# A four-layer attention network on one core: the input of the next image's layer 1 is loaded while layer 3 finishes, into a tile outside the pools that later holds similarities

## The chip, the cores and the metric

The kernel runs on one core of one Trainium2 chip. Its engines are TensorE (PE, the matmuls, with weight loads shown as PEld), VectorE (DVE), ScalarE (ACT), GpSimd (POOL) and SyncE (SP, which here only issues DMAs). The metric is the time of one execution on the device, in microseconds, smaller is better.

## The reference

The input is four images of 32 x 32 positions with 384 channels in fp32. Each image goes through four layers of the same form, `x = x + layer(gn(x))`, where gn is a group norm over 32 groups of 12 channels:

```python
x = x + _L0_conv_ref(_gn(x), ...)   # deformable attention, 6 heads of 64
x = x + _L1_conv_ref(_gn(x), ...)   # attention with group weights, 12 heads of 32
x = x + _L2_conv_ref(_gn(x))        # ratio of box sums
x = x + _L3_conv_ref(_gn(x), ...)   # outlook attention over 3 x 3 patches
```

What the change touches lies in layers 1 and 3. Layer 1 multiplies the softmax of each head by a matrix of group weights, `sim @ sim^T`, where `sim = sigmoid(...)` of the normalized products of the features xg with their strided convolution gc. Layer 3 computes nine attention vectors of nine weights for each position, applies them to the values of the 3 x 3 neighbours and folds the results back onto the image:

```python
v = image @ Wv + bv
attn = softmax((image @ Wa + ba).reshape(B, H, W, 9, 9))
win = einsum('bhwpq,bhwqc->bhwpc', attn, patches)    # patches: 3x3 windows of v
out = fold(win)                                      # 9 shifted adds
```

## The kernel before

**Two lanes.** `Front` computes layer 0, `Trunk` layers 1 to 3. Layer 0 of image 0 runs alone (about 640 us). Then `Net.layer3` (L271) drives both: the trunk works on image b and the front on image b+1. Each lane is a generator whose yields carry a number of steps; after each yield of the trunk the front is advanced until its share of the work is ahead by 0.1. This sets the order in which the program is written down. Engines take their instructions in an order that a scheduler derives from that, from the dependences and from the buffers, each engine in its own fixed order, and waits between engines are semaphores. The trunk of image 3 has no front beside it.

**Buffers.** Tiles of SBUF come from pools. `scope` opens a pool for a stretch of code; when it ends, its space is given to the next pool on that side, and whatever writes there first waits for the last reader or writer of the old tiles, transfers included. Channels stand on the 128 partitions, in KC = 3 slices of N = 1024 positions; NJ = 8 is the number of blocks of 128 positions. PSUM has two buffers `big` (1024 columns) and four `bank` (512). Weights of 384 x 384 go round in three buffers `w`.

**Norm.** `norm` (L314) takes the statistics of each slice on DVE (`stats`, L301), then sums over groups with a constant matrix gmat on PE: 14 matmuls of one column for the mean (gn_mv, L330), four small operations on DVE (L340 to L347), 14 more for the variance (gn_d, L330), Sqrt on ACT (L349), a reciprocal (L352), and the three slices of the result (L357). The dense products that follow are `dense_t` (L376, out channels on partitions) and `dense_n` (L390, positions on partitions).

**Layer 1.** `Trunk.image` (L828) opens the pool l1y (tiles q4, k4, xg), `layer1` (L838) the pool l1, in which `pair_tiles` (L975) zeroes parts of the pair tiles on POOL (L986 to L989), and then l1a for `inputs1` (L848): x is loaded by SP (L852) from x1, where the front stored it, and normed into a second tile xh. After that come the features xg (whose pads POOL zeroes at L862), queries, keys and values, which are written to DRAM, and the sums of the first pair of heads (`sums_step`, L1026; `sums_finish`, L1052, which copies a row `lrow` and stores it as `lse`, L1063). The pool l1b then holds the work of the six pairs: `sims` (L1065) computes the similarities by matmuls L1074 and sigmoids L1081 into a tile sim of 16 KB a partition; `pair` (L1090) scales them on POOL (sg, L1139), multiplies keys by queries (L1154), exponentiates (L1162), and multiplies sg by sim (L1184). `gf`/`gn` tiles keep parts for a later transpose.

**Layers 2 and 3.** `layers23` (L1217) opens the pool l23 with its own tile x, loaded by ACT's queue (L1227) from x1 again and added to layer 1's result. Layer 2 (L1256) has a tile d for each slice (L1292). Layer 3 (L1354) norms into xh, computes attention and values (L390), gathers the folded weights with selection matmuls (L1415), and writes each block's 5 x 5 window weights through DRAM (skew, L1449) so that they come back as a banded matrix mt (L1451); even blocks on SP, odd ones on ACT. Meanwhile PE transposes x in eight groups (L1460) and ACT copies each group into a tile y of its own (L1464). At the end 22 passes, the products of mt with the values (L1472, two records each in the trace), are added to y on DVE (L1480), and SP stores the eight blocks of the output (L1481). Then the next image begins.

**Front beside the seam.** Where the front works on the next image, its stores of sampled pairs (L555), dense products (L376) and grouped convolutions (L584) stand between the trunk's instructions on all engines. POOL gathers for it (L652).

The lines that set the order at the end of layer 3 and the start of layer 1:

```python
            for i in range(NJ):
                pt = self.big()
...
                y = self.wt([P, C], "y", NJ)
                nc.scalar.copy(y, pt[:, 0:C])
                ys.append(y)
            yield 20
            for i in range(NJ):
...
                nc.sync.dma_start(out[i * P : (i + 1) * P, :], y)
```

Of the kernel before, what the change touches and what calls it, by code (L numbers as in the profile page):

```python
# [26 lines left out]
P = 128  # L27
NB, HW, C = 4, 32, 384
N = HW * HW
KC = C // P  # L30
NJ = N // P
# [41 lines left out]
class Net:  # L73


    def __init__(self, ctx, tc, a):
        self.tc, self.nc, self.a = tc, tc.nc, a
        nc = self.nc
        pool = lambda name, bufs, **kw: ctx.enter_context(
            tc.tile_pool(name=name, bufs=bufs, **kw)  # L80
        )
        self.const = pool("const", 1)
        self.wts = pool("wts", 3)
        self.ps2 = pool("ps2", 2, space=PSUM)
        self.ps1 = pool("ps1", 4, space=PSUM)
        self.dram = pool("dram", 1, space=DRAM)
        self.n = 0
        self.consts()
        self.scratch()
        self.front, self.trunk = Front(self, "right"), Trunk(self, "left")  # L90

    def nm(self, base):
        self.n += 1
# [186 lines left out]
class Lane:  # L280
# [30 lines left out]
        self.stat = self.work  # L311
        return self.wt([P, KC, 2], "gn_mv", 2)

    def norm(self, x, out, mv=None):  # L314


        nc = self.nc
        if mv is None:
            mv = self.moments()
            for k in range(KC):  # L320
                self.stats(mv, x, k)
        gmat = self.weights("gmat")

        near = [[k for k in range(KC) if abs(k - ko) <= 1] for ko in range(KC)]

        def groups(src):
            ps = self.bank()
            for ko in range(KC):
                for ki in near[ko]:
                    nc.tensor.matmul(  # L330
                        ps[:, ko : ko + 1],
                        gmat[:, ki, ko * P : (ko + 1) * P],
                        src[:, ki, :],
                        start=ki == near[ko][0],
                        stop=ki == near[ko][-1],
                    )
            return ps[:, 0:KC]

        mean = self.wt([P, KC], "gn_mean")
        nc.vector.tensor_scalar(mean, groups(mv[:, :, 0:1]), 1.0 / 12.0, None, ALU.mult)  # L340
        d = self.wt([P, KC, 1], "gn_d")
        d2 = d.rearrange("p k o -> p (k o)")
        m0 = mv[:, :, 0:1].rearrange("p k o -> p (k o)")
        v0 = mv[:, :, 1:2].rearrange("p k o -> p (k o)")
        nc.vector.tensor_tensor(d2, m0, mean, ALU.subtract)
        nc.vector.tensor_tensor(d2, d2, d2, ALU.mult)
        nc.vector.tensor_tensor(d2, d2, v0, ALU.add)  # L347
        rstd = self.wt([P, KC], "gn_rstd")
        nc.scalar.activation(  # L349
            rstd, groups(d), AF.Sqrt, bias=self.eps[:, 0:1], scale=1.0 / 12.0  # L350
        )
        nc.vector.reciprocal(rstd, rstd)  # L352
        for k in range(KC):
            src = x[:, k, :]
            if len(out.shape) == 4:
                src = src.rearrange("p (y x) -> p y x", y=HW)
            nc.vector.tensor_scalar(  # L357
                out[:, k],
                src,
                mean[:, k : k + 1],  # L360
                rstd[:, k : k + 1],
                ALU.subtract,
                ALU.mult,
            )
# [460 lines left out]
class Trunk(Lane):  # L825


    def image(self, b, out):  # L828
        with self.scope("l1y"):


            self.q4, self.k4 = self.wt([P, N], "q4"), self.wt([P, N], "k4")
            self.xg = self.wt([P, N], "xg")
            yield from self.layer1(b)
            yield from self.layers23(b, out)
# [11 lines left out]

    def inputs1(self, b):  # L848
        nc, v = self.nc, self.nc.vector
        x = self.wt([P, KC, N], "x")  # L850
        for k in range(KC):
            nc.sync.dma_start(x[:, k, :], self.x1[b % 2][k * P : (k + 1) * P, :])  # L852
        xh = self.wt([P, KC, N], "xh")
        self.norm(x, xh)
        yield 15


        pads, raw = [], self.wt([P, KC, M1], "raw")
        w = self.weights("Wg")
# [52 lines left out]
        for k in range(KC):  # L912
            out = slice(32 * k, 32 * k + 32)
# [5 lines left out]
            for ps, src in ((psx[:, 0:512], 0), (psx[:, 512:N], 512), (psc[:, 0:M1], N)):  # L919
# [4 lines left out]
                    start=True,  # L924
# [18 lines left out]
        for k in range(KC):  # L943
            rows, heads = slice(k * P, (k + 1) * P), slice(32 * k, 32 * k + 32)
            ps, pc = self.big(), self.bank()
            for out, lo in ((ps[:, 0:512], 0), (ps[:, 512:N], 512), (pc[:, 0:M1], N)):
# [4 lines left out]
                    start=True,  # L951
# [113 lines left out]
    def sims(self, p):  # L1065

        nc = self.nc
        sim = self.wt([P, 2, 2, N], "sim")
        for h in range(2):
            for m in range(2):  # L1070
                ps = self.big().rearrange("p (r n) -> p r n", r=2)
                for r in range(2):
                    rows = slice(64 * r, 64 * r + 64)
                    nc.tensor.matmul(  # L1074
                        ps[:, r, :],
                        self.gc[rows, m * P : (m + 1) * P],
                        self.xg[rows, h * 512 : (h + 1) * 512],
                        start=True,
                        stop=True,
                    )  # L1080
                nc.scalar.activation(  # L1081
                    sim[:, :, m, h * 512 : (h + 1) * 512],
                    ps,
                    AF.Sigmoid,
                    bias=self.rows[:, R_SCAL + 1 : R_SCAL + 2],
                    scale=self.rows[:, R_SCAL : R_SCAL + 1],
                )
        return sim
# [127 lines left out]

    def layers23(self, b, out):  # L1217
        with self.scope("l23"):
            self.x = self.wt([P, KC, N], "x")
            yield from self.out1(b)  # L1220
            yield from self.layer2()
            yield from self.layer3(b, out)
# [33 lines left out]
    def layer2(self):  # L1256
        nc, v = self.nc, self.nc.vector
        with self.scope("l2"):
# [8 lines left out]
            def squares(k):  # L1267


                sq = self.wt([P, HW, HW + 4], "sq", 3)  # L1270
                nc.scalar.activation(sq, xp[:, k], AF.Square)

                two = self.wt([P, HW, HW + 2], "t", 2)
                v.tensor_tensor(two, xp[:, k, :, 0 : HW + 2], xp[:, k, :, 1 : HW + 3], ALU.add)
                ps = self.big()
                for h in range(2):
                    rows = slice(16 * h, 16 * h + 16)
                    for i, src in enumerate(
                        (two[:, rows, 0:HW], two[:, rows, 2 : 2 + HW], xp[:, k, rows, 4 : 4 + HW])
                    ):  # L1280
                        nc.tensor.matmul(
                            ps[:, h * 512 : (h + 1) * 512],
                            self.ident,
                            src,
                            start=i == 0,
                            stop=i == 2,
                        )
                s = self.wt([P, N], "s", KC)
                nc.scalar.activation(s, ps, AF.Square)
                num.append(s)  # L1290
                t = self.wt([P, HW, HW + 2], "t", 2)
                d = self.wt([P, HW, HW], "d", KC)  # L1292
                v.tensor_tensor(t, sq[:, :, 0 : HW + 2], sq[:, :, 1 : HW + 3], ALU.add)
                v.tensor_tensor(d, t[:, :, 0:HW], t[:, :, 2 : HW + 2], ALU.add)
                v.tensor_tensor(d, d, sq[:, :, 4 : HW + 4], ALU.add)
                for lo in (0, HW - 2):
                    e = d[:, :, lo : lo + 2]
                    v.tensor_tensor(e, e, bc(self.wnorm[:, lo : lo + 2], 1, HW), ALU.mult)
                den.append(d.rearrange("p y x -> p (y x)"))
# [54 lines left out]
    def layer3(self, b, out):  # L1354
        nc, v = self.nc, self.nc.vector
        skew = self.skew[b % 2]
        with self.scope("l3"):
# [95 lines left out]
                )  # L1453

            values(range(NJ // 2, NJ))
            ys = []
            for i in range(NJ):
                pt = self.big()
                for k in range(KC):
                    nc.tensor.transpose(  # L1460
                        pt[:, k * P : (k + 1) * P], self.x[:, k, i * P : (i + 1) * P], self.ident
                    )
                y = self.wt([P, C], "y", NJ)
                nc.scalar.copy(y, pt[:, 0:C])  # L1464
                ys.append(y)
            yield 20
            for i in range(NJ):
                ps = self.bank()
                near = [j for j in range(NJ) if abs(i - j) <= 1]
                for j in near:  # L1470
                    c0 = P * (i - j) + P
                    nc.tensor.matmul(  # L1472
                        ps[:, 0:C],
                        mt[:, j, c0 : c0 + P],
                        vals[:, j, :],
                        start=j == near[0],
                        stop=j == near[-1],
                    )
                y = ys[i]
                v.tensor_tensor(y, ps[:, 0:C], y, ALU.add)  # L1480
                nc.sync.dma_start(out[i * P : (i + 1) * P, :], y)  # L1481
                yield 4
# [84 lines left out]
```

## Time and profile before

| what | value |
| --- | --- |
| time, median of 3 runs | 4876.06 us (4868.23 to 4881.34) |
| the profiled execution: time | 4831.1 us |
| the profiled execution: span from first to last instruction | 4829.3 us |
| mean granted clock of TensorE in it | 0.91 of full speed |
| busy in the span: PE, PEld, DVE, ACT, POOL | 4189.8, 1799.4, 3132.9, 2404.9, 946.3 us |
| data moved by DMA | 366.82 MB |

The profile is of one execution. Times in it count from its first instruction. An engine's busy time is the time in which one of its instructions runs; for PE the ends of matmuls are modelled, so a busy PE can be slow. The chain of waits is followed back from the last instruction: at each step to what released it, or to the instruction before it on the same engine; a row gives start, length, engine, the tile written, the line and a count of instructions. "issue" is time in which an engine waited for nothing that the profile shows. `PEclk` is the granted clock of TensorE in tenths, in forty equal slices of the span.

By stretches of the span, PE is busy and its mean granted clock is:

| stretch, us | what | PE busy, us | clock |
| --- | --- | --- | --- |
| 0-640 | layer 0 of image 0 alone | 361.05 | 0.75 |
| 640-1787 | image 0's trunk, image 1's front | 1043.31 | 0.93 |
| 1787-1853.4 | seam 0 to 1 | 62.43 of 66.4 | 0.87 |
| 1853.4-2926.9 | image 1's trunk, image 2's front | 985.13 | 0.93 |
| 2926.9-2993.35 | seam 1 to 2 | 62.34 of 66.45 | 0.87 |
| 2993.35-4041 | image 2's trunk, image 3's front | 962.19 | 0.94 |
| 4041-4072.5 | seam 2 to 3 | 20.09 of 31.5 | 0.77 |
| 4072.5-4829.3 | image 3's trunk alone | 693.21 | 0.94 |

### The profile page before, as it was taken

The page shows a single profiled execution, that of the slowest core. Times are in us where ns is not written, and L with a number is a line of the kernel's source. Part 1 is how long each engine was busy: PE and PEld are TensorE (multiplying, and loading weights), DVE is VectorE, ACT ScalarE, POOL GpSimd, SP SyncE. Part 2 cuts the span into 40 slices and gives each one's busy share as a digit, 9 for nine tenths or more (in the row PEclk, how much of TensorE's full clock was granted, in tenths as well). Part 3 has the DMA queues.
Part 4 walks back from the last instruction along what each step waited for, and adds up shares of the span by engine and source line. Part 5 has one row for each costly group of instructions (what it writes and reads, how often), then busy time and mean ns, then how long its engine had stood idle before and what let it go on. Part 6 is the DMA issues. An engine that isn't in the chain of part 4 may idle for free.

```text
span 4829.3 us, 46659 instructions
## 1 busy us (share of the span) xinstructions
PE 4189.8 (87%) x15704; PEld 1799.4 (37%) x15704; DVE 3132.9 (65%) x5727; ACT 2404.9 (50%) x3693; POOL 946.3 (20%) x946
## 2 busy tenths in 40 slices
PE   5466678899999989889999989899999998999998
PEld 2222233333333353333333444343333335343444
DVE  3478828676877836577777762767687873454544
ACT  2155414565766513376666532457576641456642
POOL 1533303211212101421211210422121210000000
PEclk7677788999999989899999989799999998899998
DMA  6323244311212143431221224532121213201011
GB/s 118 102 84 92 70 131 144 94 53 38 80 50 73 36 147 105 126 86 50 60 62 54 65 76 113 154 92 56 33 80 42 75 45 114 87 23 33 19 39 40
DMA packets 230927, 366.82 MB, mean 76 GB/s; under 512 B 117475, under 2 KB 164672, under 8 KB 230688
## 3 DMA queue, kind: packets, MB, share of 16 engines
q1 hardware_dynamic: 169672, 197.36, 14.0%
q0 software_dynamic: 39936, 145.53, 10.3%
q10 hardware_dynamic: 21080, 20.96, 1.8%
q8 instruction: 124, 2.03, 0.2%
q14 instruction: 115, 0.94, 0.1%
HBM read 285.84 MB, written 78.21 MB: 75 GB/s over the span
## 4 chain that ended last, share of the span: by engine, by line
PE 35%; ACT 9%; DVE 7%; issue 3%; DMA 2%; POOL 0%; SPq 0%; ACTq 0%; DVEq 0%; POOLq 0%
PE bank L1184 8%; PE big L1154 4%; PE big L376 3%; PE big L1035 3%; PE bank L790 3%; PE bank L390 2%; PE bank L755 2%; PE bank L1128 2%; ACT big L1044 2%; PE bank L1179 2%; DVE e L1193 1%; DVE nmax L1043 1%; ACT e L1162 1%; PE big L1074 1%; PE bank L1472 1%
## 5 line engine op out<-in xcount | busy, mean ns | idle before, releaser
L1193 DVE SCALAR_TENSOR_TENSOR e<-bank,gam,e 128x512 f32<-128x512 f32 x768 | 557.6, 748 | 564.9 <-ACT gn L1192 275.1
L1184 PE MATMUL bank<-sim,sg 128*128 128x512 f32 (+3 forms) x2304 | 870.6, 512 | 2.8 <-DVE e L1193 2.8
L1044 ACT ACTIVATE big<-big,nmax 128x1024 f32<-128x1024 f32 x384 | 418.5, 1090 | 384.5 <-DVE nmax L1043 384.0
L734 POOL DMA_INDIRECT win<-strips,widx x384 | 425.8, 1109 | 887.4 <-DVE z L747 450.3
L1162 ACT ACTIVATE e<-big 128x1024 f32<-128x1024 f32 x384 | 376.8, 1019 | 360.2 <-PE big L1154 355.0
L1184 PEld LDWEIGHTS bank<-sim,sg 128*128 128x128 f32 x2304 | 405.9, 199 | 378.1 <-issue 297.7
L1043 DVE TENSOR_REDUCE nmax<-big 128x1 f32<-128x1024 f32 x384 | 453.1, 1217 | 54.4 <-PE big L1035 53.0
L1154 PE MATMUL big<-qa,ka 64*128 64x512 f32 x1536 | 412.1, 627 | 15.5 <-ACT big L1044 9.4
L1139 POOL TENSOR_SCALAR sg<-sim,gam 128x512 f32<-128x512 f32 x192 | 147.3, 770 | 1416.5 <-PE bank L1184 1126.9
L1035 PE MATMUL big<-k,q 32*128 32x512 f32 x1536 | 357.6, 701 | 74.5 <-ACT e L1162 37.0
L790 PE MATMUL bank<-lg,va 128*64 128x512 f32 x768 | 374.1, 634 | 44.7 <-ACT lg L788 44.6
L755 PE MATMUL bank<-qpad,kz 128*128 128x512 f32 x768 | 375.8, 620 | 22.6 <-DVE e L1193 13.7
L790 PE MATMUL bank<-lg,ones 128*64 128x512 f32 x768 | 373.4, 634 | 0.0
L746 ACT ACTIVATE z<-win,bias_f 128x528 f32<-128x528 f32 x384 | 277.0, 737 | 188.8 <-DVE lg L752 108.6
L752 DVE SCALAR_TENSOR_TENSOR lg<-z,bias_f,lg 128x512 f32<-128x512 f32 x384 | 299.9, 795 | 45.5 <-ACT lg L751 43.9
L747 DVE SCALAR_TENSOR_TENSOR z<-win,bias_f,z 128x528 f32<-128x528 f32 x384 | 291.8, 779 | 38.5 <-ACT z L746 38.1
L652 POOL DMA_INDIRECT gat<-pairs,sidx x192 | 210.8, 1098 | 448.1 <-DVE ix_gt L464 244.5
L751 ACT ACTIVATE lg<-z,bias_f 128x512 f32<-128x512 f32 x384 | 267.5, 719 | 44.1 <-DVE z L747 27.2
L787 DVE TENSOR_TENSOR lg<-lg,tb 128x512 f32<-128x512 f32 x384 | 246.2, 698 | 64.7 <-ACT tb L780 64.7
L756 DVE TENSOR_TENSOR lg<-bank,lg 128x512 f32<-128x512 f32 x384 | 256.3, 683 | 32.0 <-PE bank L755 30.7
L788 ACT ACTIVATE lg<-lg 128x512 f32<-128x512 f32 x384 | 222.4, 629 | 40.2 <-DVE lg L787 39.8
L1154 PEld LDWEIGHTS big<-qa,ka 64*128 64x128 f32 x1536 | 134.7, 188 | 272.0 <-issue 156.8
(262 smaller groups left out, 5812.2 us busy)
## 6 DMA issues: line engine op xcount, KB each, us to landing
pairs<-xn SPq DMA_DIRECT2D x64, 192.0 KB
q<-qd SPq DMA_DIRECT2D x48, 256.0 KB
w<-in_gmat SPq DMA_DIRECT2D x16, 576.0 KB
w<-in_w_off SPq DMA_DIRECT2D x12, 576.0 KB
w<-in_Wqkv SPq DMA_DIRECT2D x12, 576.0 KB
a<-in_x SPq DMA_DIRECT2D x16, 384.0 KB
x<-a ACTq DMA_DIRECT2D x4, 1536.0 KB
k<-a SPq DMA_DIRECT2D x12, 512.0 KB
```

The lines of the kernel that those rows point to most:

```text
L734: nc.gpsimd.indirect_dma_start(out=win, out_offset=None, in_=self.strips[:, :], in_offset=bass.IndirectOffsetOnAxis(ap=self.widx[:, q, c : ...
L747: v.scalar_tensor_tensor(z, wv[:, 1 : HH + 1, 0 : HW + 1], sc(0, 1), z, ALU.mult, ALU.add)
L752: v.scalar_tensor_tensor(lg, z[:, :, 1 : HW + 1], sc(0, 0), lg, ALU.mult, ALU.add)
L755: nc.tensor.matmul(ps, kz[:, j * P : (j + 1) * P], both, start=True, stop=True)
L790: nc.tensor.matmul(po[out, :], w, lf, start=j == 0, stop=j == NJ - 1)
L1035: nc.tensor.matmul(ps[r][:, h * 512 : (h + 1) * 512], self.q4[rows, i * P : (i + 1) * P], self.k4[rows, 0:512], start=True, stop=True,)
L1043: v.tensor_reduce(nmax[:, r, i : i + 1], ps[r], AX.X, ALU.max, negate=True)
L1044: nc.scalar.activation(ps[r], ps[r], AF.Exp, bias=nmax[:, r, i : i + 1], accum_out=den[:, r, i : i + 1],)
L1154: nc.tensor.matmul(ps[:, r, :], ka[rows, j * P : (j + 1) * P], qa[rows, cols], start=True, stop=True,)
L1162: nc.scalar.activation(e, ps, AF.Exp)
L1184: nc.tensor.matmul(ps[:, (mid - i0) * P :], sg[:, r, m, :], sim[:, r, m, mid * P : i1 * P], start=m == 0, stop=m == 1,)
L1193: v.scalar_tensor_tensor(e[:, r, :], ps, self.gam[:, 1:2], e[:, r, :], ALU.add, ALU.mult, accum_out=tot[:, r, h : h + 1],)
```

## The change

A pool `keep` with one buffer is opened on the trunk's side before all scopes. It holds one tile `whole` of 16 KB a partition, which serves in turn:

- `start(b)` loads x of image b into three quarters of it (SP) and loads gmat. For image 0 this happens at the head of `image`, for the others in layer 3 of the image before, after the transposes of x (the `yield 20`) and before the products.
- At the head of `image`, before the pool l1y is opened, x is normed in place, with the gmat that `start` loaded. The tiles x and xh of `inputs1` are gone.
- `sims` writes the similarities of each pair into the same tile, once the normed x has been read for the last time.
- `layers23` takes three quarters of it as x and the fourth as the third tile d of layer 2.

In layer 3 the eight tiles y are gone: the transposed blocks go into a second tile of the tag xh, so into the buffer that the normed x of layer 3 has.

```diff
--- before.py
+++ after.py
@@ -88,6 +88,7 @@
         self.consts()
         self.scratch()
         self.front, self.trunk = Front(self, "right"), Trunk(self, "left")
+        self.trunk.work = self.trunk.keep = pool("keep", 1, side="left")
 
     def nm(self, base):
         self.n += 1
@@ -311,7 +312,7 @@
         self.stat = self.work
         return self.wt([P, KC, 2], "gn_mv", 2)
 
-    def norm(self, x, out, mv=None):
+    def norm(self, x, out, mv=None, gmat=None):
 
 
         nc = self.nc
@@ -319,7 +320,8 @@
             mv = self.moments()
             for k in range(KC):
                 self.stats(mv, x, k)
-        gmat = self.weights("gmat")
+        if gmat is None:
+            gmat = self.weights("gmat")
 
         near = [[k for k in range(KC) if abs(k - ko) <= 1] for ko in range(KC)]
 
@@ -825,7 +827,28 @@
 class Trunk(Lane):
 
 
+    def whole(self):
+
+
+        work, self.work = self.work, self.keep
+        t = self.wt([P, 4 * N], "whole")
+        self.work = work
+        return t, t[:, 0 : KC * N].rearrange("p (k n) -> p k n", k=KC)
+
+    def start(self, b):
+
+        x = self.whole()[1]
+        for k in range(KC):
+            self.nc.sync.dma_start(x[:, k, :], self.x1[b % 2][k * P : (k + 1) * P, :])
+        self.begun = x, self.weights("gmat")
+
     def image(self, b, out):
+        if b == 0:
+            self.start(b)
+        x, gmat = self.begun
+        self.norm(x, x, None, gmat)
+        self.xh = x
+        yield 15
         with self.scope("l1y"):
 
 
@@ -847,13 +870,7 @@
 
     def inputs1(self, b):
         nc, v = self.nc, self.nc.vector
-        x = self.wt([P, KC, N], "x")
-        for k in range(KC):
-            nc.sync.dma_start(x[:, k, :], self.x1[b % 2][k * P : (k + 1) * P, :])
-        xh = self.wt([P, KC, N], "xh")
-        self.norm(x, xh)
-        yield 15
-
+        xh = self.xh
 
         pads, raw = [], self.wt([P, KC, M1], "raw")
         w = self.weights("Wg")
@@ -1065,7 +1082,7 @@
     def sims(self, p):
 
         nc = self.nc
-        sim = self.wt([P, 2, 2, N], "sim")
+        sim = self.whole()[0].rearrange("p (r m n) -> p r m n", r=2, m=2)
         for h in range(2):
             for m in range(2):
                 ps = self.big().rearrange("p (r n) -> p r n", r=2)
@@ -1216,7 +1233,8 @@
 
     def layers23(self, b, out):
         with self.scope("l23"):
-            self.x = self.wt([P, KC, N], "x")
+            whole, self.x = self.whole()
+            self.spare = whole[:, KC * N :].rearrange("p (y x) -> p y x", y=HW)
             yield from self.out1(b)
             yield from self.layer2()
             yield from self.layer3(b, out)
@@ -1289,7 +1307,7 @@
                 nc.scalar.activation(s, ps, AF.Square)
                 num.append(s)
                 t = self.wt([P, HW, HW + 2], "t", 2)
-                d = self.wt([P, HW, HW], "d", KC)
+                d = self.wt([P, HW, HW], "d", 2) if k < 2 else self.spare
                 v.tensor_tensor(t, sq[:, :, 0 : HW + 2], sq[:, :, 1 : HW + 3], ALU.add)
                 v.tensor_tensor(d, t[:, :, 0:HW], t[:, :, 2 : HW + 2], ALU.add)
                 v.tensor_tensor(d, d, sq[:, :, 4 : HW + 4], ALU.add)
@@ -1453,17 +1471,19 @@
                 )
 
             values(range(NJ // 2, NJ))
-            ys = []
+
+            ys = self.wt([P, KC, N], "xh").rearrange("p k (a c) -> p (k a) c", c=P)
+            ys = ys.rearrange("p (i k) c -> p i (k c)", k=KC)
             for i in range(NJ):
                 pt = self.big()
                 for k in range(KC):
                     nc.tensor.transpose(
                         pt[:, k * P : (k + 1) * P], self.x[:, k, i * P : (i + 1) * P], self.ident
                     )
-                y = self.wt([P, C], "y", NJ)
-                nc.scalar.copy(y, pt[:, 0:C])
-                ys.append(y)
+                nc.scalar.copy(ys[:, i], pt[:, 0:C])
             yield 20
+            if b + 1 < NB:
+                self.start(b + 1)
             for i in range(NJ):
                 ps = self.bank()
                 near = [j for j in range(NJ) if abs(i - j) <= 1]
@@ -1476,7 +1496,7 @@
                         start=j == near[0],
                         stop=j == near[-1],
                     )
-                y = ys[i]
+                y = ys[:, i]
                 v.tensor_tensor(y, ps[:, 0:C], y, ALU.add)
                 nc.sync.dma_start(out[i * P : (i + 1) * P, :], y)
                 yield 4

```

## The prediction

> **What bounds the kernel.** I read the page first, then the chain of waits in stretches around the places that the diff touches, and where the chain was not enough, single instructions of the trace. The page:
>
> ```profile
> span 4829.3 us, 46659 instructions
> ...
> PE 4189.8 (87%) x15704; PEld 1799.4 (37%) x15704; DVE 3132.9 (65%) x5727; ACT 2404.9 (50%) x3693; POOL 946.3 (20%) x946
> ...
> PE   5466678899999989889999989899999998999998
> PEclk7677788999999989899999989799999998899998
> ```
>
> PE is busy 87% of the span, and nearly full after the first five slices (640 us, layer 0 of image 0 alone). A change that touches no product can win only where PE waits or runs at a lower clock. There are three seams between images, at about 1787-1853, 2926-2993 and 4039-4072 us. The last has no front lane beside it. Its chain:
>
> ```profile
> 4032.33 6.64 DMA mt<-skew
> ...
> 4039.11 0.88 PE bank L1472 x2
> ...
> 4041.62 12.91 PE bank L1472 x40
> ...
> 4055.22 1.85 DMA out<-y
> ...
> 4064.24 2.85 PE bank L330 x12
> ...
> 4067.91 3.16 PE bank L330 x14
> ...
> 4072.47 7.66 PE big L376 x14
> ```
>
> The products end at 4054.5 and the first dense product of the next image starts at 4072.5: 18.0 us in which PE does only two groups of tiny matmuls. In between stand the last output's transfer (SP's loads of x wait until its buffer is free), the loads of x (issued 4057.28, landed 4061.05), three times the statistics, gn_mv (the first L330 group), four small DVE operations, gn_d (the second), Sqrt, reciprocal and xh.
>
> The seam 1→2, with the front lane beside it (0→1 is the same to 0.1 us):
>
> ```profile
> 2926.92 10.30 PE big L376 x24
> 2937.22 7.89 PE big L584 x72
> 2945.11 11.16 PE bank L1472 x34
> ...
> 2972.01 4.11 issue
> 2976.12 0.47 PE bank L330 x2
> 2976.60 1.91 PE big L584 x8
> ...
> 2985.05 3.08 PE bank L330 x14
> 2988.12 5.30 PE big L584 x20
> 2993.42 6.63 PE big L376 x15
> ```
>
> Here the front's dense and convolution cover the mt transfers, and the products follow when mt has landed. From the end of the values (2926.9) to the dense on xh (2993.4) are 66.4 us. PE waits 4.1 us for x and its statistics (the "issue" row), and after that wait it is slow: the third convolution takes 4.43 + 1.91 + 1.91 + 1.89 + 5.30 = 15.4 us in place of 7.89, four of its matmuls 0.85 us in place of 0.43. So 4.1 + 7.5, less the small steps that stay, about 11.2 us are there to be won, and 55.2 are work.
>
> **The change, part by part.** The order of the changed program's instructions tells what stands behind what; durations are of the profiled execution (4831.1 us, span 4829.3). It lies 45 us, 0.9%, below the median 4876.06, so differences are found on it and taken off the median. About 0.3% (14.6 us) is what a measurement can tell from no change.
>
> *Seam 2→3.* In the changed order SP issues the loads of x behind the first output, once the transposes have read the old x (about 4042), so they land long before 4055. The statistics lie between the y adds on DVE; ACT loads the Sqrt table during the products. After the products remain gn_mv, mean and d, gn_d, Sqrt, reciprocal and the first xh. Now these take 8.2 us from 4064.2, the 28 tiny matmuls at 0.215 us each. Where the same 28 follow full work, in the norm of layer 3 at 3993.66, their first and last start are 4.8 us apart (0.113 each, and the wait for d), in place of 7.7 at 4063.00. I take 4.8 + 1.8 (last gn_d to dense, 4070.71 to 4072.47) = 6.6. Against that, y now lies in xh's buffer, so ACT's copies wait until the values have read xh; before, three of the eight groups of transposes stood behind mt's landing, now six. Three more at 0.33 us give +1.0; products end at 4055.5, dense starts at 4062.1: **10.4 gained**. Bounds: 8.7 with the matmuls at their slow pace, 12 if dense starts at the full pace too (its first three passes now take 2.7 us, not 1.3). Writing in place costs DVE nothing: 0.75 us a slice as before. POOL's zeroing of pair tiles and pads (4057.38 to 4065.7, once the outputs have landed) ends about 1 us later, 4066.7; ACT needs the pads after six passes, 4066.0, and PE the buffer that ACT then frees only after twelve, 4068.6. That hides it, thinly: if POOL is 2 us later still, its lateness is paid.
>
> *Seams 0→1 and 1→2.* The sharing of xh's buffer puts eight copies on ACT behind the values, and behind four skew and four mt issues on ACT's queue. On PE the order becomes values, one group of transposes, product 0, the other transposes mixed with products 0 and 1, and only then the front's dense. So product 0's wait for mt is no longer covered. Before, SP issued mt j=0 at 2929.05 and it landed at 2933.64 (4.6 us). Six groups of transposes less ahead of the skew bring the issue earlier, by 1.9 us on PE at most; the front's stores of pairs ahead of it on SP let through about 1.25 (estimate between 0 and 1.9). Product 0 starts at about 2932.6, 3.6 us of transposes and products stand before the front's dense: 2936.2 in place of 2926.9. From there the work has no hole: dense 10.4, three convolutions 3 × 7.89, remaining products 12.5, gn_mv and gn_d 6.3, small steps 0.6, together 53.5, and 2989.7 against 2993.35: 3.6. The 28 tiny matmuls at the fast pace give 2 more; the new hole before product 0, some 7 us, costs clock. What it costs has two rows: after the wait at 4072.47 three passes are slow, 1.4 us; after the one at 2972 it lasts 17 us and costs 7.5. Products resemble the dense, so I take 2, and **3.6 gained**; for 0→1, with mt j=0 issued at 1788.63, by the same sum dense on xh at 1849.0 against 1853.4, **4.4 gained**. Bounds: with mt as slow as in the last seam (6.64 us) and issued no earlier, 3.1 less; with the long slow clock, 5.5 less; with mt 0.6 earlier still and the clock's cost at 1.4, 1.2 more.
>
> [...]
>
> *Pair 0 of layer 1.* The similarities now lie outside the pools, so they needn't wait until the inputs' pool is given back. Before, in image 3:
>
> ```profile
> 4181.80 1.98 DMA lse<-lrow
> ...
> 4183.94 1.28 ACT L1081
> 4185.24 1.21 ACT sim L1081
> ```
>
> ACT's Sigmoid table waits for lse, whose landing freed the pool. Changed, the table load and the first sigmoid stand ahead of the copy to lrow, at 4180.85: 3.1 us earlier, less 0.3 for the copy in between. lse lands some 1.8 us later, at 4185.6, before L1154 needs it (4187.5). Gain **2.7**, bounds 0 to 4. In images 0 to 2 the wait is longer (lse 5.49 us at 3118.00), but there POOL scales the similarities right behind the front's gathers, and PE's products L1184, which now stand ahead of L1154, wait for POOL. I take **0**, with −1 to +1.5 each, for the three.
>
> *The end.* In the last image six groups of transposes stand behind mt as well (4810.32), and nothing follows to win it back: **+1.0**, bounds 0.5 to 2.
>
> *At no cost.* ACT's loads of the residual x (L1227) wait for the last reader of the similarities, about 2.3 us later than 4676.20; DVE needs the first at 4689.51, after a transfer of some 4 us, so 7 us cover it. The third d lies in the spare quarter with its reader and writer in order. Image 0 starts as before. The counts on PE, ACT and POOL are equal.
>
> Sum: −4.4 − 3.6 − 10.4 − 2.7 + 0 + 1.0 = −20.1, so **4856 us**.
>
> **The rivals.**
>
> *A: only the last seam gains.* Where the front lane runs, the new hole and its slow clock take what is won: 0 there. For it: the hole of 7 us is longer than the wait it replaces. Against: mt's own rows. −10.4 − 2.7 + 1 = −12, and with pair 0 worth nothing −9: 4864 to 4867.
>
> *B: slower, by the wait for mt.* The front seams' transfers compete with the front's stores (DMA share 0.82 in 1780-1800). If product 0 waits as long as mt's last issue of before plus 6.64 us (2933.03 + 6.64 = 2939.7; 1793.35 + 6.64 = 1800.0) and the slow clock lasts 17 us, dense on xh comes at 2939.7 + 3.6 + 53.5 + 5.5 = 3002.3, a loss of 9, and as much at 0→1. It decides once product 0 starts later than 2936.3 and 1796.5, or 2 us sooner with the long slow clock. With pair 0 of images 0 to 2 at +1.5 each and no gain in image 3: 18 + 4.5 + 1 − 10.4 = +13, 4889; to +23 if POOL then holds up the last seam as well.
>
> *C: it does not do what it says.* x is early, but the norm itself stays behind all products in PE's order. That is in the sum: 6.6 of 18 us stay. Were the statistics late as well, behind the last y add (4055.7), three of them at 1.4 us would follow: 4856 + 4 = 4860.
>
> **Chances.** Forecast (−15 to −30) 0.50; A 0.23; C 0.12; B 0.15. Faster by over 0.3%: the forecast and a little of C, 0.52. Slower by over 0.3%: the upper half of B, 0.09. Within: 0.39. The range: the best bounds, 4.8 + 5.6 + 12 + 4 + 3 − 0.5 = 29 below, give 4847; above I go to the middle of what lies between A and B, 4878.
>
> **What would show it.** In the changed trace: the x loads issued 10 us or more before the last product of image 2; 6 to 8 us from that product to the next L376; a hole of about 7 us on PE before product 0 near 2932 and 1792, and none before gn_mv; the third convolution at 7.9 us; the sigmoid ahead of lrow's copy. Wrong I am if product 0 waits over 11 us, if the clock stays low behind that hole, if POOL or a weight load stands before the dense in the last seam, or if pairs in layer 1 become longer.

## The result and the profile after

The changed kernel takes 4861.99 us (median of 12 runs, 4849.3 to 4886.91), the kernel before, run beside it, 4871.31 us (12 runs, 4860.06 to 4883.48). The ratio is 0.9983, 95% interval 0.9967 to 0.9998: about 8 us faster, with 1 to 16 in the interval. That lies within 0.3% of no change and inside the range, and is 8 of the 20 us that were forecast.

The two profiled executions can't be compared by their spans: the one of before (4829.3) lies 40 us under the median of its kernel, the one of after hardly under its own.

```profile
span 4855.3 us, 46679 instructions
...
PE 4194.5 (86%) x15704; PEld 1801.7 (37%) x15704; DVE 3139.1 (65%) x5727; ACT 2406.1 (50%) x3693; POOL 952.3 (20%) x946
```

The counts of each engine are equal and the busy times nearly so; nothing is to be read from this page. What can be compared are stretches between the same two instructions. I use four marks in each image: the first dense product on the normed x of layer 1, the first product of the similarities, the first product of keys and queries in pair 0, and the first tiny matmul of layer 3's norm. All are start times of PE's instructions in the traces.

| stretch, us, images 0 / 1 / 2 / 3 | before | after |
| --- | --- | --- |
| dense on xh to similarities | 119.7 / 120.8 / 120.8 / 105.8 | 135.5 / 132.7 / 128.1 / 107.5 |
| similarities to keys and queries | 15.9 / 15.9 / 16.2 / 11.8 | 20.3 / 20.7 / 20.4 / 11.8 |
| layer 3's norm to the next dense on xh (seams) | 120.2 / 119.7 / 78.8 | 115.8 / 115.4 / 67.9 |
| layer 3's norm to the end of the span (end) | 67.0 | 67.3 |

**The last seam** first. The chain of waits of the changed kernel between 4070 and 4110 us (start, length, what):

```profile
4071.34 6.37 DMA mt<-skew
...
4077.84 0.88 PE bank L1492 x2
...
4081.98 12.26 PE bank L1492 x38
4094.24 1.47 PE bank L332 x14
...
4096.54 2.07 PE bank L332 x14
...
4100.40 9.62 PE big L378 x17
```

The products end at 4094.24 and gn_mv starts in the same moment: no output, load or statistics stands between. The 14 matmuls of gn_mv take 1.47 us, those of gn_d 2.07, in place of 2.85 (for twelve of them) and 3.16; the granted clock is 1.00 and 0.80 in them, where it was 0.50 in both before. From the end of the products to the dense product are 6.2 us in place of 17.9; six groups of transposes (L1480) stand among the first products in place of three.

Two small costs lie behind this mark. The granted clock is 0.50 from 4100.4 to 4104.6, where the dense product runs five slow passes (0.86 us each); before, it had three, at 0.50 from 4072.4 to 4075.2. And the norm's three slices on DVE, now written while POOL zeroes the pair tiles, take 3.35 us in place of 2.26. From the dense product to the similarities image 3 needs 107.5 us in place of 105.8.

**The seam 1→2**, chain of the changed kernel, 2948 to 2975 us:

```profile
2959.29 4.29 DMA mt<-skew
...
2963.71 1.62 PE bank L1492 x2
2965.33 1.28 PE big L1480 x6
...
2969.61 5.58 PE big L378 x13
```

This is the new hole. The values end at 2958.0; but for one group of transposes PE does nothing until mt lands at 2963.6. The front's dense product comes 9.8 us later against the stretch before it, as the sum had it (9.3). The first two products take 1.62 us and six transposes 1.28, where the last seam has 0.88 and 0.66: the granted clock is 0.50 from 2963.7 to 2967.9 and 1.00 in those rows of the last seam, and about 2.1 us are lost against them. What follows then has no wait, and the seam is 4.3 us shorter all the same.

**Pair 0.** The view of waits for the stretch 2005 to 2032 us of the changed kernel, image 1 (who waited for whom: us, times, longest):

```profile
POOL gat L654 <- DMA lse<-lrow: 9.5, 1, 9.5
...
PE bank L1201 <- POOL sg L1156: 4.6, 1, 4.6
```

Here the gain is given back. POOL's queue stands at the first of six gathers of the front, which run from 2014.59 to 2024.00; only then comes sg. (The view puts the wait of that gather down to lse; in images 0 and 2, and in the kernel before, it names xn on DVE.) Single instructions, first of the kernel before, then of the changed one:

```profile
1990.03 1.37 POOL L1139 TENSOR_SCALAR sg<-sim,gam 128x512 f32<-128x512 f32 x2
1990.12 1.99 PE L1154 MATMUL big<-qa,ka 64*128 64x512 f32 x8
1992.03 3.70 PE L1184 MATMUL bank<-sim,sg 128*128 128x512 f32 x8
...
2024.00 1.37 POOL L1156 TENSOR_SCALAR sg<-whole,gam 128x512 f32<-128x512 f32 x2
2024.76 3.78 PE L1201 MATMUL bank<-whole,sg 128*128 128x512 f32 x4 [4.58 <-POOL sg L1156]
2028.46 2.38 PE L1171 MATMUL big<-qa,ka 64*128 64x512 f32 x8
```

Before, the six gathers took as long (1980.66 to 1990.03), but the similarities ended with them (1989.6); keys and queries followed at once, beside sg on POOL, and the products with sg behind them ran at a granted clock of 1.00 (eight in 3.70 us). Now the similarities end at 2019.7, and PE's next instruction is L1201, which needs sg. PE is idle for 4.6 us and then computes four such products in 3.78 us, at a granted clock of 0.50; keys and queries come behind them. Over the whole span of the changed kernel:

```profile
PE bank L1201 <- POOL sg L1156: 14.7, 3, 6.4
```

Three times, one in each of images 0 to 2 (6.4, 4.6 and 3.7 us); in the kernel before only the weight loads waited for sg there, 2.3 us in all three. "Similarities to keys and queries" overstates the loss, since four products have moved ahead of the second mark. Up to the first product of the next pair's sums PE has done the same work in both kernels: 21.5 / 21.5 / 21.8 us before, 24.1 / 24.9 / 25.4 changed, so 9.5 us are lost in the three images.

### The profile page after: what moved, and what is told of

Its sections match the earlier page's. It is cut to its first block, busy times and chain, and to the rows that moved or that the text cites. A ratio compares the mean times of both kernels' runs of the same rounds, so it can differ in the third digit from the quotient of the medians.

```text
span 4855.3 us, 46679 instructions
## 1 busy us (share of the span) xinstructions
PE 4194.5 (86%) x15704; PEld 1801.7 (37%) x15704; DVE 3139.1 (65%) x5727; ACT 2406.1 (50%) x3693; POOL 952.3 (20%) x946
## 4 chain that ended last, share of the span: by engine, by line
PE 36%; ACT 8%; DVE 6%; issue 3%; DMA 2%; POOL 1%; SPq 0%; ACTq 0%; DVEq 0%; POOLq 0%
PE bank L1201 8%; PE big L1171 4%; PE big L1052 3%; PE big L378 3%; PE bank L792 3%; PE bank L757 2%; PE bank L1145 2%; PE bank L392 2%; ACT big L1061 2%; PE bank L1196 2%; DVE e L1210 1%; DVE nmax L1060 1%; PE big L1324 1%; ACT e L1179 1%; PE bank L1492 1%
## 5 line engine op out<-in xcount | busy, mean ns | idle before, releaser
L1201 PE MATMUL bank<-whole,sg 128*128 128x512 f32 (+3 forms) x2304 | 878.6, 515 | 17.4 <-POOL sg L1156 14.7
L1201 PEld LDWEIGHTS bank<-whole,sg 128*128 128x128 f32 x2304 | 407.6, 200 | 396.8 <-issue 302.4
L1156 POOL TENSOR_SCALAR sg<-whole,gam 128x512 f32<-128x512 f32 x192 | 147.1, 769 | 1418.2 <-PE bank L1201 1142.7
```

The source lines that it names most:

```text
L1201: nc.tensor.matmul(ps[:, (mid - i0) * P :], sg[:, r, m, :], sim[:, r, m, mid * P : i1 * P], start=m == 0, stop=m == 1,)
```

## The experiments

Theory: the seams and image 3 gain what the sum says, and pair 0 of images 0 to 2 loses some 10 us through the order on PE ("POOL order"). Rival: the loss is the stretch before it (first row of the table, 7 to 16 us an image), which the change lengthens by its loads or its order on POOL ("inputs"). Below, "sums" stands for the time from the first product of the similarities to the first of the next pair's sums, in images 0 to 3. The runs fell on several chips, on which the kernel before took 4839 us in one and 4865 in another; each ratio is against runs of it on the same chip.

**The kernel before, twice more.** No edit.

> The kernel before, once more, for a second profile. The first profile of it lay 40 us under its median, that of the changed kernel 5 us under its own. In the first pair of profiles the stretch of layer 1 from the first dense product on the normed x to the first product of the similarities took 120.8 us before and 132.7 us after in image 1, 120.9 and 128.1 in image 2. Theory 'variation': the long stretch belongs to runs, not to the change, so this profile shows 125 to 135 us too, and a span near 4860. Rival 'inputs': the change slows this stretch itself, by its loads or by the order on POOL, so this profile shows 121 us again.

Measured: 4841.97 us, and 119.9 / 120.7 / 120.8 us for the stretch. That left the question open, since the time as a whole was short here too. The third:

> The kernel before, a third profile. In eight profiles of the changed kernel and its variants the stretch of layer 1 from the first dense product on the normed x to the first product of the similarities took 120 to 121 us in images 0 to 2 where the kernel before, run beside them, had a median of 4839 us, and mostly 125 to 135 us where it had 4865 to 4871. Theory: the long stretch goes with the chip or the hour, not with the kernel, so the kernel before shows it too when its own time is near 4865, and 120 us when it is near 4840. Rival: it belongs to the changed order, and the kernel before shows 120 us at any of its times.

Measured: 4850.75 us, and 124.6 / 120.2 / 134.6. The kernel before has the long stretch too, in two of three images.

**The changed kernel again.** No edit.

> The changed kernel once more, on the chip and beside the kernels it is compared with. Theory: ratio 0.998; the stretch from the first dense product on the normed x to the first product of the similarities, which took 128 to 136 us in its first profile and 120 to 121 in five others, two of them of kernels with the same order on PE up to there, was a matter of that run and is 120 to 121 here; from there to the first product of keys and queries 20 us in images 0 to 2, as in the first profile. Rival: the long stretch belongs to the change and is there again.

Measured: ratio 0.9979 [0.9964, 0.9994]. The long stretch is there again (135.1 / 133.7 / 130.8), against the theory's 120; similarities to keys and queries 20.7 / 20.6 / 21.3; seams 115.7, 116.1, 70.4; sums 24.5 / 24.6 / 26.3 / 15.0.

**The similarities of pair 0 wait again.**

```diff
+        bias = self.rows[:, R_SCAL + 1 : R_SCAL + 2]
+        if p == 0:
+            late = self.wt([P, 1], "late")
+            nc.scalar.copy(late, bias)
+            bias = late
...
-                    bias=self.rows[:, R_SCAL + 1 : R_SCAL + 2],
+                    bias=bias,
```

The tile `late` lies in the pool of the pairs, l1b.

> The changed kernel, but in the first pair of each image the sigmoids wait again until the pool of the inputs is given back (their bias is copied into that pool's successor). On PE the products of keys and queries then stand ahead of sg times sim again, as before the change. Theory 'POOL order': in images 0 to 2 the changed order makes PE wait for sg, which stands behind the front's gathers on POOL, and costs some 4.5 us an image, so this kernel is 10 us faster than the changed one (ratio to before about 0.996), with image 3's gain of 3 us lost. The time from the first product of the similarities to the first of keys and queries is back at 16 us from 20 to 22 in images 0 to 2. Rival 'inputs': the loss lies ahead of the similarities, this kernel is at 0.998 like the changed one.

Measured: 0.997 [0.9959, 0.9982]; similarities to keys and queries 15.3 / 15.9 / 16.0 / 12.2; dense to similarities 119.8 / 121.3 / 121.4; sums 20.9 / 21.4 / 21.6 / 18.9. The loss in images 0 to 2 is gone from the trace, and image 3's gain with it. The ratio moved less than was expected, and its interval overlaps the changed kernel's; by the sums, 10 us come back and 3 go.

**The first sg of pair 0 on VectorE.**

```diff
-            nc.gpsimd.tensor_scalar(
+            (v if p == 0 and j == 0 else nc.gpsimd).tensor_scalar(
```

> The changed kernel, with the first sg of each image's first pair made on VectorE instead of POOL; PE's order is the changed one, to the instruction. Theory 'POOL order': sg no longer stands behind the gathers, keys and queries start 4 to 6 us earlier in images 0 to 2, ratio to before 0.995 to 0.996. Rival 'inputs': no change against the changed kernel, 0.998.

Measured: 0.9958 [0.9942, 0.9975]; similarities to keys and queries 15.9 / 15.8 / 16.1, sums 19.7 / 19.6 / 19.9 / 15.7, and the wait of L1201 for sg is gone from the list. PE's order is the changed kernel's, instruction by instruction; only the engine of one operation is another. So it was sg's place on POOL, and neither early similarities nor PE's order by themselves. That dense to similarities took 119.9 / 119.8 / 121.4 here, with all engines' orders but for sg itself as in the changed kernel, speaks against "inputs" as well.

**Own tiles for the transposed blocks.**

```diff
-            ys = self.wt([P, KC, N], "xh").rearrange("p k (a c) -> p (k a) c", c=P)
-            ys = ys.rearrange("p (i k) c -> p i (k c)", k=KC)
+            spare = self.spare.rearrange("p y x -> p (y x)")
+            ys = [spare[:, i * C : (i + 1) * C] for i in range(2)]
+            ys += [self.wt([P, C], "y", NJ - 2) for _ in range(NJ - 2)]
...
```

The copies and the additions then use `ys[i]`.

> The changed kernel, with the transposed blocks of layer 3 in tiles of their own again (two of them in the spare quarter), so that PE transposes before the values and the front's dense products follow the values at once; the early load stays. Theory 'mt hole': the hole of 7 us before the first product in the seams 0 to 1 and 1 to 2 is gone and comes back nowhere, since x and its statistics are early; the dense product on the normed x comes 5 to 8 us earlier in each of the two seams, ratio about 0.995. Rival: the hole only moves, to a wait for mt after the front's convolution or for x before the tiny matmuls, and the two seams stay as they are (0.998).

Measured: 0.9926 [0.991, 0.9942]; layer 3's norm to the next dense 106.6 and 105.8 (changed kernel 115.8 and 115.4). The chain of this kernel around seam 1→2:

```profile
2916.53 0.70 PE big L1481 x5
2917.22 0.64 PE bank L1444 x4
2917.86 7.74 PE bank L392 x24
2925.60 10.30 PE big L378 x24
2935.90 7.89 PE big L586 x72
2943.79 11.16 PE bank L1493 x34
```

The transposes (L1481) stand ahead of the values again, the front's dense product follows the values at once and hides mt. The hole does not move elsewhere: it cost 9 to 10 us in each of the two seams. Of these 5.7 are the hole and 2.1 the slow clock behind it; I put the rest, not measured apart, down to the transposes, which here run in other waits of PE, ahead of the values. I had expected 5 to 8. Pair 0 still loses (similarities to keys and queries 20.4 / 20.3 / 20.3, sums 25.1 / 25.2 / 25.2).

**The early load undone.**

```diff
+        if b > 0:
+            self.nc.vector.tensor_copy(x[:, :, 0:1], self.last[:, 0:KC].unsqueeze(2))
```

with the call of `start` at the head of `image`, and `self.last` the last block of the output, so that the loads wait for the last addition.

> The changed kernel with the early load undone: three elements of the tile are first copied from the last block of the output on VectorE, so that the loads of x can be issued only after the last addition; tile, norm in place and all else as in the changed kernel. Theory: the early load is what the seams gain from, so the wait before the statistics and the slow clock behind it come back; from layer 3's norm to the next dense product 126 us or more in the seams 0 to 1 and 1 to 2 (changed: 115.6) and 76 to 78 in the last (changed: 67.9); ratio to before about 1.004. Rival: the front's work hides the load in the first two seams, 116 to 118 there and ratio about 1.000.

Measured: 1.0054 [1.0033, 1.0074]; seams 125.6 / 127.2 / 79.7. All three come back, the first two by 10 and 12 us. In the seam 1→2 the wait stands in the list again:

```profile
DVE gn_st L307 <- DMA whole<-x: 4.6, 1, 4.6
```

So the front did not hide the load in the first two seams, and the whole change without it would be a loss of 0.5%.

**The loads at the head of the next image.**

```diff
-            if b + 1 < NB:
-                self.start(b + 1)
```

and `start(b)` at the head of `image` for each b.

> The changed kernel, but the loads stand in the program at the head of the next image, behind the products and outputs, not ahead of them; the tile outside the pools stays. The scheduler issues them early all the same, behind the first output, since nothing but the transposes holds the tile. Theory 'tile': what counts is that the tile is outside the pools, so that its loads wait for no output; ratio 0.998, seams as in the changed kernel to 1 us. Rival 'place': the place in the program counts, the seams lose 5 us or more each.

Measured: 0.9967 [0.9953, 0.9982]; seams 115.9 / 115.3 / 70.8. The place in the program does nothing: once the tile lies outside the pools, the scheduler puts the loads behind the first output by itself (one of the three behind the second, in the last seam).

**Both repairs.** Own tiles for the blocks, and the first sg on VectorE (the two diffs above).

> Both repairs: transposed blocks in tiles of their own, and the first sg of each image's first pair on VectorE. Theory: the two losses are independent, so the gains add: the two first seams 106 us from layer 3's norm to the next dense product, 16 us from the similarities to keys and queries, ratio to before about 0.990 (0.9926 less some 12 us). Rival: they share a wait, 0.9926 as with the first repair alone.

Measured: 0.9901 [0.9878, 0.9924], against 0.9979 for the changed kernel on the same chip; seams 106.2 / 106.2 / 68.9, similarities to keys and queries 14.2 / 13.6 / 13.7, sums 18.0 / 17.4 / 17.5. In the trace the two gains add up. This version has the lowest ratio: 1% faster than the kernel before, where the change alone has 0.2%. Its first products with sg start 0.43 us apart, those of the run with sg on VectorE alone 0.85.

## Why the prediction was half right

| term | forecast, us | first profiles, us | other profiles with this part as in the change |
| --- | --- | --- | --- |
| seam 0→1 | −4.4 | −4.4 | −4.5 to −2.1 |
| seam 1→2 | −3.6 | −4.3 | −4.4 to −3.6 |
| seam 2→3 | −10.4 | −10.9 | −10.9 to −8.0 |
| image 3, pair 0 (sums) | −2.7 | −2.4, with two more products done by then | −3.8 to −2.4 |
| image 3, dense to similarities | not in the sum | +1.7 | +1.0 to +2.0, 0.0 with the early load undone |
| images 0 to 2, pair 0 (sums) | 0 (−3 to +4.5) | +2.6 + 3.4 + 3.5 = +9.5 | +8.7 to +10.6 |
| the end | +1.0 | +0.3 | +0.6 to +4.0 |
| sum | −20.1 | −10.5 | |

The differences of the last column are against the first profile of before. The sum of the measured terms lies 2 us from what the ratio says (0.17% of 4871 us is 8.3, interval 1 to 16). It leaves out the stretch from the dense product to the similarities in images 0 to 2, on which more below.

**Right:** what bounds the seams; that in the last seam POOL's zeroing comes in time for PE (60 passes of the dense products follow one another without a gap, 4100.4 to 4128.4) and that the loads of the residual cost nothing (it is added 13.6 us behind the last product with sg in images 0 to 2 of both kernels); the fast pace of the tiny matmuls behind the products (28 in 4.2 us from first to last start, at granted clocks of 1.00 and 0.80, taken as 4.8 from a row in which the clock was 0.50 from 3996.8 on); the new hole, put at 7 us and 5.7 long, with product 0 at 2963.71, which is 2931 on the clock of the kernel before (estimated 2932.6); and its price in clock, put at 2 and measured at 2.1. It was right to take the row of the dense products for that and not the 17 us row.

**Wrong** is the term for pair 0 of images 0 to 2: "there POOL scales the similarities right behind the front's gathers, and PE's products L1184, which now stand ahead of L1154, wait for POOL. I take **0**, with −1 to +1.5 each". The facts in that sentence hold, but they were costed as if only the time of sg counted, and sg comes when it came before (15.9, 16.2 and 15.9 us behind the first similarity; before 15.9, 15.8 and 16.1). It left out what PE does until then and at which clock it goes on. Keys and queries, which need no sg, now stand behind it in PE's fixed order and can't fill the time; PE is idle for 3.7 to 6.4 us, and four products follow at a granted clock of 0.50 to 0.53. With the same work done that is 2.6 to 3.5 us an image, about twice its upper bound, in three images. The same question asked of the seams, what stands behind the waiting instruction, had given the right answer there.

Too good was also "Writing in place costs DVE nothing: 0.75 us a slice as before". It is so in image 0 (0.81 us an instruction in both kernels), but in the three seams, where the slices now run beside POOL's zeroing, they take 0.88 to 1.58 us, and in the last seam the dense product waits 0.3 us longer for the first.

The size of the gain in the third convolution was a little too good: it still takes 10.5 us for 72 matmuls beside the tiny ones, with a granted clock of 0.83 in the last 68 (15.4 before; 7.9 behind the dense product, at 1.00). That the seam 1→2 still came within 0.7 us of its term is partly luck: the convolution was 2.6 us longer than in the sum, product 0 came 1.7 us earlier, and the 28 tiny matmuls took 3.1 us where 4.3 were left for them.

**The rivals:** A (only the last seam gains) fell, both front seams gain 4 us; but the number it gave, 4864 to 4867, is nearer to the result than the forecast's, for another reason. B (slower, by the wait for mt) fell: product 0 came 5 us before the point from which it decides, in both seams. C (statistics late) fell: gn_mv follows the last product without a gap.

**Open:** the stretch from the dense product to the similarities takes 120 us in some profiles and up to 135 in others. The kernel before has both (119.7 to 134.6), and kernels with one and the same order have both, so it isn't shown to belong to the change. The ratios speak against it as well: with both repairs the other terms add up to −50 us and the ratio says −48 (37 to 59), though the stretch was 31 us longer there than in the first profile of before. So the kernel before should have the long stretch on that chip too, but no profile of it from there was taken. Still, the changed kernel itself was long in both its profiles, in six of six images, and what sets the length was not found. POOL's gathers wait longer for VectorE there (42.8 us in all in the second profile of the changed kernel, 8.2 in the one with sg on VectorE).

## What to carry to other kernels

Here a buffer that came free earlier let work start earlier, and the scheduler put that work earlier in PE's fixed order: in pair 0 of images 0 to 2 the products with sg ahead of keys and queries, and PE then waited 3.7 to 6.4 us for sg. Ask for each moved instruction not only when its input is ready, but what now stands behind it and could have run while it waits. A tile outside nested pools was enough to let a load slip ahead of the outputs; where it stands in the program didn't matter here (the first two seams took 115.9 and 115.3 us with the loads at the head of the next image, 115.7 and 116.1 in the changed kernel on the same chip). Where two tiles are made to share a buffer to pay for it, look at what the sharing orders: here it cost 9 to 10 us at each of two places, more than the seam gained.

## What the runs showed of the hardware

The granted clock behind two holes on PE, first in the changed kernel, then in the kernel before (the figure behind POOL's count is the clock):

```profile
2963.70:2967.90 4.20, 4.19 (x12) 2.77 (x13) 0.00 (x0) 0.96 (x2) 0.00 (x0) 0.50 0.64 192
...
2976.10:2993.30 17.20, 17.18 (x66) 8.32 (x66) 5.72 (x14) 1.55 (x2) 2.70 (x10) 0.50 0.13 38
```

Behind the hole of 5.7 us in the changed kernel (2958.0 to 2963.7, with one group of transposes of 0.55 us in it) the products and transposes ran at a granted clock of 0.50 for 4.2 us; from 2967.9 to 2972 it was 0.99. In the kernel before, behind a wait of 4.1 us, convolutions with 64 by 64 weights between tiny matmuls ran at 0.50 for 17.2 us, and the clock was 1.00 from 2993.4 to 3000, in the dense product. The two stretches differ in the wait ahead of them and in what PE computed, and no run changes one of these alone, so what set their length was not shown. In the last seam of the changed kernel PE has nothing but tiny matmuls from 4094.2 to 4100.4, with no wait over 1.8 us; the clock is 1.00 in the first 14 of them, 0.80 in the other 14, 0.79 on average over the stretch, and 0.50 from 4100.4 to 4104.6.

In the seams of the changed kernel slices of the norm on DVE, which ran there beside POOL's zeroing, took 0.88 to 1.58 us, in place of 0.81 in the kernel before, and some of the zeroing instructions 1.39 to 1.49 us in place of 0.94.

One and the same kernel differed by 0.5% between two chips (4839 and 4865 us for the kernel before, medians of 16 and 23 runs), more than most of the terms above.
